# Reordered first loads, head rows written after a logarithm, and more norm tiles in a gated two-layer block

## The chip, the cores and the metric

The kernel runs on one core of a Trainium2 chip. The metric is the device time of one execution in microseconds (us), and the median of several executions is compared. A core has five engines that run side by side, each with an instruction stream of its own that it takes in order: TensorE (PE in the profile, with its weight loads as PEld), VectorE (DVE), ScalarE (ACT), GpSimd (POOL) and SyncE (SP). SP, ACT and POOL can also issue DMA transfers, each into a queue of its own; 16 DMA engines do the moving for all of them.

## What is computed

The input x has 32 samples of 128 tokens with 128 features, and so has the context. Four updates are added to x one after the other, each behind a layer norm:

```
x = x + tanh(g_xattn[0]) * mlstm(layernorm(x), ctx, ctx, ifgate_w, ifgate_b, outnorm_w)
x = x + tanh(g_ffn[0])   * quantized_ffn(layernorm(x), W1, b1, W2, b2)
x = x + tanh(g_xattn[1]) * time_warp_align(ctx, layernorm(x))
x = x + tanh(g_ffn[1])   * gated_experts(layernorm(x), gate_weight, w1, b1, w2, b2)
```

Only the first one matters here. Its gates and its decay matrix are

```
pre    = 15 * tanh((concat[q, k, v] @ ifgate_w.T + ifgate_b) / 15)     # i_pre, f_pre for 8 heads
lf     = cumsum(log_sigmoid(f_pre))
log_d  = lf[t] - lf[s] + i_pre[s]            for s <= t, else -inf
d_mat  = exp(log_d - max_s log_d)
h      = (q k^T / 4 * d_mat) v / max(|row sum|, exp(-m))
```

q is the normed x, and k and v are both the context, so the gate weights of k and v can be summed first.

## The kernel before

The token (or the feature) lies on the 128 partitions; X holds x with tokens on partitions, CT the context in the same way, CD the context with features on partitions, and YT the transposed normed x. Each of X, CT and CD is 2 MB and is loaded in four quarters of eight samples (512 KB each) by `quarter` (L91). So X0 stands for the quarter with samples 0 to 7, X1 for 8 to 15, and so on.

**Loads (L94 to L115).** SP issues X0, CD0, X2, CD2, then CT0, CT1, CD3, CT2, CT3, and then eight small or middle-sized parameters. ACT issues gx (the two gates of the attention updates), X1, wg (the gate weights), gb (the gate biases), gf (the two gates of the feed-forward updates), CD1 and X3. POOL issues none of the first loads.

**Constants.** GpSimd fills masks and small rows; `later_constants` (L129) makes rev, ones, onesb and magic_c. VectorE adds the gate weights of k and v into wkv (L375). ACT takes the tanh of gx and gf (L142, L144), copies an identity pattern to ind (L353), and writes W (L377) from wg and wkv and rows (L382) from gb. TensorE turns the rows into the bias columns cols (L390, L395) and forms the 0/1 head rows hrow (L401, L405).

**Norm.** `norm_steps` (L192) takes n samples: statistics with one BATCH_NORM_STATS2 for each sample (L154), combination and three Newton steps for the reciprocal root (L159 to L189), then for each sample a normed tile y (L210, four tile buffers) that TensorE transposes (L214). After four samples the transposed group is copied to YT (L366 in the first norm, where two groups share a tile of PSUM). `first_norm(0)` does samples 0 to 15, `first_norm(1)` samples 16 to 31.

**Gates.** `gate_steps(r)` (L428) does 16 samples: gate products of W with CD and YT (L437), two tanh (L442), Exp (L443), Ln (L445), a scan for the cumulative sum (L450), g (L455), a scan for the running maximum (L458), a split of the maximum and of g into bf16 parts (L412 to L418, L470), and a DMA of the maximum to DRAM (L464). RH[r] is the right-hand side of the decay product. Four copies, one for each of four samples, fill it with hrow (L407 for r = 0, before the gates; L635 for r = 1, after all steps of the gates), and then `running_max(r)` (L421) overwrites three of its rows in each group of 32 by four DMAs from DRAM, two on SP and two on POOL.

**Attention.** For each sample n, `scores` multiplies CD with qm (L508; qm is YT masked per head, L498), `decays` multiplies GP with RH (L524) and takes the exponential (L529), and `values` multiplies both (L551) and applies them to va (L554). The gates of samples 16 to 31 and the weights' quantization run beside the first samples, a step at a time, through `paced(rest_of_gates())`. `with tc.issue_after(ins)` puts what is written in the block behind `ins` in the order of that instruction's engine; otherwise the tile framework fixes each engine's order at compile time from the order of the program and its own estimate of when an operand is ready.

Of the kernel before, what the change touches and what calls it, by code (L numbers as in the profile page):

```python
# [8 lines left out]
F32 = mybir.dt.float32  # L9
# [9 lines left out]
P = 128  # L19
B = 32  # L20
S = 128
D = 128
NH = 8
# [5 lines left out]
GB = 4  # L29
# [9 lines left out]
def tile_flamingo_gated(  # L39
# [21 lines left out]
    nc = tc.nc  # L61
# [5 lines left out]
    def new(p, shape, dt, tag, bufs=None):  # L67
        kw = {} if bufs is None else {"bufs": bufs}
        return p.tile(shape, dt, tag=tag, name=tag, **kw)
# [5 lines left out]
    X = new(keep, [P, B, D], F32, "X")  # L75
    CT = new(keep, [P, B, D], F32, "CT")
    CD = new(keep, [P, B, S], F32, "CD")
    wg = new(keep, [P, 3, 2 * NH], F32, "wg")
    gb = new(keep, [P, 2 * NH], F32, "gb")
    onw = new(keep, [P, D], F32, "onw")  # L80
    gx = new(keep, [P, 2], F32, "gx")
# [9 lines left out]
    def quarter(queue, to, src, q):  # L91
        queue.dma_start(out=to[:, 8 * q : 8 * q + 8, :], in_=src[:, 8 * q : 8 * q + 8, :])

    for q in (0, 2):  # L94
        quarter(nc.sync, X, x, q)
        quarter(nc.sync, CD, ctx_d, q)
    nc.scalar.dma_start(out=gx, in_=g_xattn.to_broadcast([P, 2]))
    quarter(nc.scalar, X, x, 1)
    nc.scalar.dma_start(out=wg, in_=ifg_w)
    nc.scalar.dma_start(out=gb, in_=ifg_b.to_broadcast([P, 2 * NH]))  # L100
    nc.scalar.dma_start(out=gf, in_=g_ffn.to_broadcast([P, 2]))
    quarter(nc.scalar, CD, ctx_d, 1)
    quarter(nc.scalar, X, x, 3)
    for q in range(4):
        quarter(nc.sync, CT, ctx_t, q)
        if q == 1:
            quarter(nc.sync, CD, ctx_d, 3)
    nc.sync.dma_start(out=onw, in_=outnorm_w.to_broadcast([P, D]))
    nc.sync.dma_start(out=w1s, in_=w1)
    nc.sync.dma_start(out=w2s, in_=w2)  # L110
# [18 lines left out]
    def later_constants():  # L129

        nc.gpsimd.memset(rev, 1.0)
        nc.gpsimd.affine_select(
            out=rev, in_=rev, compare_op=ALU.is_equal, fill=0.0, base=1 - P,
            pattern=[[1, P]], channel_multiplier=1,
        )
        nc.gpsimd.memset(ones, 1.0)
        nc.gpsimd.memset(onesb, 1.0)
        nc.gpsimd.memset(magic_c, MAGIC)
# [8 lines left out]
    held = {}  # L147
# [44 lines left out]
    def norm_steps(p, psp, s0, n, take, tag, shape=None):  # L192

        xq = X[:, s0 : s0 + n, :]
        m, w = (8, "") if n <= 8 else (16, "_w")
        mean = new(p, [P, m], F32, "bn_mean" + w)[:, 0:n]
        r = new(p, [P, m], F32, "bn_r" + w)[:, 0:n]
        for _ in row_norm_steps(p, xq, n, mean, r):
            yield
        for h in range(n // GB):  # L200
            if shape is None:
                tp = new(psp, [P, GB, S], F32, tag)
            else:
                if h % 2 == 0:
                    pair = new(psp, shape, F32, tag)
                tp = pair[:, h % 2]
            for i in range(GB):
                j = GB * h + i
                y = new(p, [P, D], F32, "y", bufs=4)
                got = nc.vector.tensor_scalar(  # L210
                    y, xq[:, j, :], mean[:, j : j + 1], r[:, j : j + 1], ALU.subtract, ALU.mult
                )
                held["y"] = getattr(got, "ins", got)
                nc.tensor.transpose(tp[:, i, :], y, ident)  # L214
                if i % 2 == 1:
                    yield
            take(s0 // GB + h, tp)
            yield
# [70 lines left out]
    with ExitStack() as st:  # L289
        ap = pool(st, "attn")  # L290
        gp = pool(st, "gates")
# [39 lines left out]
        for k in range(2):  # L331
            nc.gpsimd.affine_select(
                out=mtmp[:, k], in_=mtmp[:, k], compare_op=ALU.is_ge, fill=0.0, base=-64 * k,
# [3 lines left out]
                out=mtmp[:, k], in_=mtmp[:, k], compare_op=ALU.is_ge, fill=0.0,  # L337
# [7 lines left out]
            out=mneg, in_=mneg, compare_op=ALU.is_ge, fill=-BIG, base=0,  # L345
            pattern=[[0, 4], [1, P]], channel_multiplier=-1,
        )
        small_c = new(ap, [P, 1], F32, "small_c")
        nc.gpsimd.memset(small_c, 5e-8)
        later_constants()  # L350

        ind = new(ap, [NH, NH, S], BF16, "ind")
# [3 lines left out]
        RH = [new(ap, [P, NH, GB, S], BF16, f"RH{r}") for r in range(2)]  # L356
# [14 lines left out]
            sel[:, :, 0:3, :],  # L371
            identb[0:NH, 0:NH].unsqueeze(1).unsqueeze(1).to_broadcast([NH, R4, 3, NH]),
        )
        wkv = new(gp, [P, 2 * NH], F32, "wkv")
        nc.vector.tensor_add(wkv, wg[:, 1, :], wg[:, 2, :])  # L375
        for k, w in enumerate((wg[:, 0, :], wkv)):
            nc.scalar.copy(  # L377
                W[:, k, :, 0:24].rearrange("p f (c h) -> p f c h", h=NH),
# [19 lines left out]
        hrow = new(gp, [P, NH, S], BF16, "hrow")  # L398
        for k in range(2):
# [3 lines left out]
                rhs=ind[:, 4 * k : 4 * k + 4, :], start=True, stop=True,  # L403
            )
            nc.scalar.copy(hrow[:, 4 * k : 4 * k + 4, :], hr_ps)  # L405
        for i in range(GB):
            nc.scalar.copy(RH[0][:, :, i, :], hrow)  # L407

        def three_parts(v, out_to):

# [10 lines left out]
        def running_max(r):  # L421
            for j in range(R4):
                (nc.sync, nc.gpsimd)[j % 2].dma_start(
                    out=RH[r][HW * j + 24 : HW * j + 27].rearrange("k h i t -> k (h i t)"),
                    in_=m_dram[r, HW * j : HW * j + 24].rearrange("(k h) i t -> k (h i t)", h=NH),
                )

        def gate_steps(r):  # L428

            sp = new(gp, [P, GB * S], F32, "sp", bufs=2)  # L430
            th = new(gp, [P, GB * S], F32, "th", bufs=2)
            for f, to, bias in ((1, sp, bias_f), (0, th, bias_i)):
                ps = new(p_at, [P, GB * S], F32, "at")
                for k, src in ((1, CD), (0, YT)):
                    for j in range(R4):
                        b = 16 * r + 4 * j
                        nc.tensor.matmul(  # L437
                            ps[HW * j : HW * j + HW, :], lhsT=W[:, k, f, :],
                            rhs=src[:, b : b + 4, :].rearrange("p b s -> p (b s)"),
                            start=(k == 1), stop=(k == 0),  # L440
                        )
                nc.scalar.activation(to, ps, AF.Tanh, bias=bias, scale=1.0 / 15.0)  # L442
            nc.scalar.activation(sp, sp, AF.Exp, scale=-15.0)  # L443
            yield
            got = nc.scalar.activation(sp, sp, AF.Ln, bias=one_c)  # L445
            held["Ln", r] = getattr(got, "ins", got)
            yield

            cs = new(gp, [P, GB * S], F32, "cs", bufs=2)
            nc.vector.tensor_tensor_scan(  # L450
                cs, first0.rearrange("p i t -> p (i t)"), sp, 0.0, ALU.mult, ALU.add
            )
            yield
            g = th
            nc.vector.scalar_tensor_tensor(g, th, 15.0, cs, ALU.mult, ALU.add)  # L455
            yield
            mx = sp
            nc.vector.tensor_tensor_scan(  # L458
                mx, firstn.rearrange("p i t -> p (i t)"), g, -BIG, ALU.add, ALU.max
            )  # L460
            yield
            for _ in three_parts(mx, MP[:, r, :]):
                yield
            nc.sync.dma_start(out=m_dram[r].rearrange("p i t -> p (i t)"), in_=MP[:, r, :])  # L464
            if r == 0:
                running_max(0)
            gx3 = new(gp, [P, GB * S], F32, "gx3")
            for _ in three_parts(g, gx3):
                yield
            got = nc.vector.tensor_scalar(GP[:, r, :], gx3, keep24, neg3, ALU.mult, ALU.add)  # L470
            held["GP", r] = getattr(got, "ins", got)
            yield

            nc.vector.tensor_sub(cs, cs, mx)
            yield
            em_ps = new((p_bi, p_at)[r], [P, GB, P], F32, ("bi", "at")[r])
            for i in range(GB):
                nc.tensor.transpose(em_ps[:, i, :], cs[:, S * i : S * i + S], ident)
            yield
            nc.scalar.activation(  # L480
                EM[:, r].rearrange("p i j c -> p (i j c)"),
                em_ps.rearrange("p i c -> p (i c)"), AF.Exp,
            )
# [147 lines left out]
        def rest_of_gates():  # L631
            for _ in second:
                yield True
            for i in range(GB):
                nc.scalar.copy(RH[1][:, :, i, :], hrow)  # L635
                yield True
            running_max(1)
            nc.vector.tensor_scalar(gain, onw, 1.0, tgx[:, 0:1], ALU.add, ALU.mult)
            yield True
            for _ in weight_steps(hp, p_at, "at"):  # L640
                yield True
# [215 lines left out]
    with ExitStack() as st:  # L857
# [51 lines left out]
        for r0, n in CHUNKS:  # L909
            dc = new(wp, [H2, 16, S], F32, "dc")[:, 0:n, :]  # L910
            for v in (slice(0, 4), slice(4, n)) if r0 == 0 else (slice(0, n),):
                for h in range(2):
                    queues[h].dma_start(
                        out=dc[B * h : B * h + B, v], in_=d_dram[h, :, r0 + v.start : r0 + v.stop, :]
# [22 lines left out]
            for q in range(2):  # L937
                for h in range(2):
                    queues[h].dma_start(
                        out=rb[H2 * q + B * h : H2 * q + B * h + B, 0 : m + 1],  # L940
                        in_=ru[B * h : B * h + B, q * m : q * m + m + 1],
# [25 lines left out]
            for q in range(2):  # L967
                queues[q].dma_start(
                    out=DV[:, r0 + q * m : r0 + q * m + m, :], in_=dv[H2 * q : H2 * q + H2]
# [208 lines left out]
```

## Time and profile before

| | us |
|---|---|
| Median of 3 runs | 926.87 (925.89 to 928.11) |
| Profiled execution, its own time | 924.18 |
| Its span | 922.5 |
| First memset to the first decay product (L524) | 51.36 |
| End of the first Ln (L445) | 33.37 |
| Attention stage, to the last YT copy | about 200 |
| Dense and distance stages | about 200 to 318 |
| Time-warp stage | about 318 to 440 |
| Experts | about 440 to 922 |
| One head-row copy (L407 or L635) | 1.04 |

The page gives the busy share of each engine (PE 75%, DVE 62%, ACT 42%, POOL 2%) over the whole span. The stages have different limits, so a share says little about one place; the windows and the timeline of the first 80 us say more.

### The profile page before, as it was taken

The page shows a single profiled execution, that of the slowest core. Times are in us where ns is not written, and L with a number is a line of the kernel's source. Part 1 is how long each engine was busy: PE and PEld are TensorE (multiplying, and loading weights), DVE is VectorE, ACT ScalarE, POOL GpSimd, SP SyncE. Part 2 cuts the span into 40 slices and gives each one's busy share as a digit, 9 for nine tenths or more (in the row PEclk, how much of TensorE's full clock was granted, in tenths as well). Part 3 has the DMA queues.
Part 4 walks back from the last instruction along what each step waited for, and adds up shares of the span by engine and source line. Part 5 has one row for each costly group of instructions (what it writes and reads, how often), then busy time and mean ns, then how long its engine had stood idle before and what let it go on. Part 6 is the DMA issues. An engine that isn't in the chain of part 4 may idle for free.

```text
span 922.5 us, 11329 instructions
## 1 busy us (share of the span) xinstructions
PE 690.1 (75%) x4026; PEld 443.6 (48%) x4026; DVE 568.5 (62%) x1987; ACT 384.7 (42%) x647; POOL 18.0 (2%) x50
## 2 busy tenths in 40 slices
PE   3699999624266400001999999999999999999998
PEld 1223333211044300001777776777777777777776
DVE  5857888869988399978656355897322322322232
ACT  3667665469365300000434444433443343344332
POOL 2000000000400000000000000000000000000000
PEclk9789999855557755555899999999999999999999
DMA  8000000040002435410000000000000000000000
GB/s 303 33 2 11 1 1 1 0 183 0 0 1 47 88 80 111 91 31 0 1 1 1 1 1 1 1 12 24 1 1 12 1 12 1 1 12 1 12 1 12
DMA packets 12081, 25.25 MB, mean 27 GB/s; under 512 B 2528, under 2 KB 7392, under 8 KB 11232
## 3 DMA queue, kind: packets, MB, share of 16 engines
q1 hardware_dynamic: 9448, 18.62, 6.8%
q10 hardware_dynamic: 2448, 5.81, 2.5%
q8 instruction: 31, 0.51, 0.2%
q14 instruction: 26, 0.21, 0.1%
q0 software_dynamic: 128, 0.10, 0.0%
HBM read 14.02 MB, written 4.46 MB: 20 GB/s over the span
## 4 chain that ended last, share of the span: by engine, by line
PE 51%; DVE 22%; issue 2%; ACT 2%; DMA 1%; ACTq 0%; DVEq 0%; POOLq 0%
PE mpo L1108 24%; PE mph L1099 21%; DVE ru L929 3%; DVE hit L975 2%; DVE hst L754 2%; DVE hst L755 2%; DVE ru L928 2%; DVE bn L154 1%; PE d L823 1%; PE po L809 1%; PE d L825 1%; PE small L1039 1%; DVE pt L1023 1%; PE px L1026 1%; PE px L1035 1%
## 5 line engine op out<-in xcount | busy, mean ns | idle before, releaser
L1108 PEld LDWEIGHTS mpo<-mw2s,hT 128*128 128x128 f32 x2048 | 252.2, 192 | 62.6 <-issue 39.2
L1102 ACT ACTIVATE hT<-mph,mb1s 128x512 f32<-128x512 f32 x256 | 175.9, 687 | 237.6 <-PE mph L1099 236.0
L1108 PE MATMUL mpo<-mw2s,hT 128*128 128x128 f32 x2048 | 256.4, 276 | 0.1
L1099 PE MATMUL mph<-YT,mw1s 128*128 128x512 f32 x512 | 243.1, 597 | 0.0
L1087 DVE SCALAR_TENSOR_TENSOR X<-mpo,GA,X 128x128 f32<-128x128 f32 x192 | 54.0, 343 | 198.1 <-PE mpo L1108 198.1
L1099 PEld LDWEIGHTS mph<-YT,mw1s 128*128 128x128 f32 x512 | 87.6, 192 | 61.6 <-issue 61.5
L1087 DVE SCALAR_TENSOR_TENSOR X<-mb2s,GA,X 128x128 f32<-128x128 f32 x256 | 73.1, 342 | 0.0
L882 PE MATMUL gt_ps<-ident,ru 32*128 32x32 f32 x1 | 0.3, 283 | 79.5 <-DVE ru L929 79.5
L551 DVE TENSOR_TENSOR sm<-sc,dm 128x512 f32<-128x512 f32 x64 | 43.6, 684 | 17.3 <-ACT dm L529 17.3
L529 ACT ACTIVATE dm<-bi 128x512 f32<-128x512 f32 x64 | 37.9, 597 | 30.3 <-PE bi L524 24.1
L508 PE MATMUL sc<-qm,CD 64*128 64x512 f32 x128 | 41.3, 652 | 0.0
L882 PEld LDWEIGHTS gt_ps<-ident,ru 32*128 32x128 f32 x1 | 0.2, 178 | 79.6 <-issue 79.6
L965 ACT COPY dv<-vv 128x8 bf16<-128x8 bf16 (+1 forms) x5 | 1.1, 220 | 79.8 <-DVE vv L961 79.8
L554 PE MATMUL at<-sm,va 128*32 128x128 f32 x512 | 28.5, 287 | 5.0 <-DVE sm L551 3.7
L929 DVE TENSOR_TENSOR_SCAN ru<-ru,dc 64x128 f32<-64x128 f32 x64 | 26.7, 417 | 6.7 <-DMA dc<-d_dram 4.7
L745 PE MATMUL ph<-XQ,w1q 128*128 128x512 bf16 x32 | 15.8, 615 | 17.2 <-ACT HT L750 7.7
L523 PE MATMUL bi<-mneg,identb 128*128 128x512 bf16 x64 | 25.7, 401 | 1.9 <-ACT dm L529 1.5
L809 PE MATMUL po<-w2q,hqt 128*128 128x128 bf16 x128 | 13.0, 280 | 17.9 <-DVE hqt L804 17.9
L1036 ACT COPY YT<-px 128x512 f32<-128x512 f32 x8 | 4.7, 585 | 50.5 <-PE px L1035 50.5
L803 ACT ACTIVATE hqt<-HT,low 128x2048 bf16<-128x2048 f32 x8 | 15.8, 1998 | 22.9 <-DVE low L700 13.3
L524 PE MATMUL bi<-RH,GP 32*128 32x512 bf16 x64 | 24.7, 388 | 0.0
L554 PEld LDWEIGHTS at<-sm,va 128*32 128x32 f32 x512 | 10.6, 108 | 29.2 <-DVE sm L551 9.1
(303 smaller groups left out, 843.5 us busy)
## 6 DMA issues: line engine op xcount, KB each, us to landing
CT<-in_ctx_t SPq DMA_DIRECT2D x4, 512.0 KB, 7.6
mw1s<-in_mw SPq DMA_DIRECT2D x1, 2048.0 KB, 8.0
mw2s<-in_mw SPq DMA_DIRECT2D x1, 2048.0 KB, 13.5
out_x<-X SPq DMA_DIRECT2D x8, 256.0 KB, 2.0
d_dram<-dist SPq DMA_DIRECT2D x15, 128.0 KB, 2.4
rblk<-ru ACTq DMA_DIRECT2D x6, 297.0 KB, 4.1
rblk<-ru SPq DMA_DIRECT2D x6, 297.0 KB, 4.8
CD<-in_ctx_d SPq DMA_DIRECT2D x3, 512.0 KB, 8.1
```

The lines of the kernel that those rows point to most:

```text
L508: nc.tensor.matmul(scs[:, k], lhsT=CD[kr, n, :], rhs=qm[kr, :, n % GB, :], start=True, stop=True)
L523: nc.tensor.matmul(bi, lhsT=identb, rhs=mneg, start=True, stop=False)
L524: nc.tensor.matmul(bi, lhsT=GP[jr, r, S * i : S * i + S], rhs=RH[r][jr, 4 * hf : 4 * hf + 4, i, :], start=False, stop=True,)
L529: done = nc.scalar.activation(dm, bi, AF.Exp)
L551: got = nc.vector.tensor_tensor(sm, held["sc", n][:, hf], held.pop(("dm", n, hf)), ALU.mult)
L554: last = nc.tensor.matmul(at[HW * c : HW * c + HW, 2 * (n % 2) + hf, :], lhsT=va[:, n % 8 * NH + 4 * hf + c, :], rhs=sm[:, c, :], start=Tr ...
L809: nc.tensor.matmul(po[:, i, :], lhsT=hq[:, c, i * S : (i + 1) * S], rhs=w2q[:, c, :], start=(c == 0), stop=(c == NC - 1),)
L929: nc.vector.tensor_tensor_scan(ru[:, r + 1, 0, 1 : S + 1], u, dc[:, r, :], BIG, ALU.min, ALU.add)
L1087: nc.vector.scalar_tensor_tensor(X[:, b, :], v, gate, X[:, b, :], ALU.mult, ALU.add)
L1099: nc.tensor.matmul(ph, lhsT=mw1s[:, e, c * P : (c + 1) * P], rhs=tok, start=True, stop=True)
L1102: nc.scalar.activation(hT[:, c, :], ph, AF.Gelu_apprx_tanh, bias=mb1s[:, e, c : c + 1])
L1108: nc.tensor.matmul(po[:, i, :], lhsT=hT[:, c, i * S : (i + 1) * S], rhs=mw2s[:, e, c, :], start=(c == 0), stop=(c == NC - 1),)
```

## The change

- ACT issues wg, gb, gx and gf first and then X1, and no other load. SP issues X0, CD0, X2, CT0, CD2, CT1, CT2, CT3 and then its parameters as before. POOL issues CD1, X3 and CD3.
- The sum wkv is made by GpSimd instead of VectorE. In the program it stands between POOL's second and third load.
- The copies of hrow into RH[r] stand inside `gate_steps`, tied behind that half's Ln on ACT, for both halves; `running_max(r)` follows the DMA of the maximum in both halves.
- y in `norm_steps` has eight tile buffers instead of four.

```
-    for q in (0, 2):
-        quarter(nc.sync, X, x, q)
-        quarter(nc.sync, CD, ctx_d, q)
-    nc.scalar.dma_start(out=gx, in_=g_xattn.to_broadcast([P, 2]))
-    quarter(nc.scalar, X, x, 1)
     nc.scalar.dma_start(out=wg, in_=ifg_w)
     nc.scalar.dma_start(out=gb, in_=ifg_b.to_broadcast([P, 2 * NH]))
+    nc.scalar.dma_start(out=gx, in_=g_xattn.to_broadcast([P, 2]))
     nc.scalar.dma_start(out=gf, in_=g_ffn.to_broadcast([P, 2]))
-    quarter(nc.scalar, CD, ctx_d, 1)
-    quarter(nc.scalar, X, x, 3)
-    for q in range(4):
+    quarter(nc.scalar, X, x, 1)
+    quarter(nc.sync, X, x, 0)
+    quarter(nc.sync, CD, ctx_d, 0)
+    quarter(nc.sync, X, x, 2)
+    quarter(nc.sync, CT, ctx_t, 0)
+    quarter(nc.sync, CD, ctx_d, 2)
+    for q in range(1, 4):
         quarter(nc.sync, CT, ctx_t, q)
-        if q == 1:
-            quarter(nc.sync, CD, ctx_d, 3)
...
-                y = new(p, [P, D], F32, "y", bufs=4)
+                y = new(p, [P, D], F32, "y", bufs=8)
...
         nc.gpsimd.memset(small_c, 5e-8)
+        quarter(nc.gpsimd, CD, ctx_d, 1)
+        quarter(nc.gpsimd, X, x, 3)
+        wkv = new(gp, [P, 2 * NH], F32, "wkv")
+        nc.gpsimd.tensor_add(wkv, wg[:, 1, :], wg[:, 2, :])
+        quarter(nc.gpsimd, CD, ctx_d, 3)
         later_constants()
...
-        wkv = new(gp, [P, 2 * NH], F32, "wkv")
-        nc.vector.tensor_add(wkv, wg[:, 1, :], wg[:, 2, :])
...
-        for i in range(GB):
-            nc.scalar.copy(RH[0][:, :, i, :], hrow)
...
             held["Ln", r] = getattr(got, "ins", got)
             yield
+            with tc.issue_after(held["Ln", r]):
+                for i in range(GB):
+                    nc.scalar.copy(RH[r][:, :, i, :], hrow)
+                    yield
...
-            if r == 0:
-                running_max(0)
+            running_max(r)
...
             for _ in second:
                 yield True
-            for i in range(GB):
-                nc.scalar.copy(RH[1][:, :, i, :], hrow)
-                yield True
-            running_max(1)
```

## Prediction

> **What bounds the kernel now.** I read the page's busy shares first (TensorE leads with 75% of the span), then the chain that ended last: half of it is the expert stage after 440 us, which no edit touches. The edits lie in the first 77 us, so I read that stretch by windows, by the timeline and by the list of waits.
>
> Windows (us; busy time and count of PE, PEld, DVE, ACT, POOL; TensorE clock, DMA share, GB/s), in two answers:
>
> ```profile
> 0.00:5.00 5.00, 0.00 (x0) 0.00 (x0) 3.31 (x2) 0.00 (x0) 4.37 (x27) 1.00 0.46 97
> 5.00:10.00 5.00, 0.00 (x0) 0.00 (x0) 1.23 (x6) 0.00 (x0) 0.51 (x4) 1.00 0.91 330
> 10.00:15.00 5.00, 0.13 (x1) 0.13 (x1) 3.58 (x21) 3.24 (x8) 0.00 (x0) 1.00 0.97 378
> ...
> 33.37:40.00 6.63, 2.28 (x8) 1.41 (x8) 6.59 (x14) 6.60 (x11) 0.00 (x0) 0.63 0.00 0
> 40.00:51.30 11.30, 10.02 (x23) 3.20 (x22) 5.93 (x19) 3.46 (x6) 1.22 (x2) 0.61 0.07 22
> 51.30:61.00 9.70, 9.70 (x75) 3.00 (x74) 3.31 (x5) 6.33 (x10) 0.00 (x0) 1.00 0.00 1
> 61.00:69.00 8.00, 6.60 (x41) 1.91 (x33) 7.06 (x14) 7.25 (x13) 0.00 (x0) 0.80 0.01 2
> 69.00:77.00 8.00, 7.30 (x63) 2.79 (x62) 7.74 (x17) 7.50 (x12) 0.21 (x1) 0.98 0.05 16
> ```
>
> Until 10 us nothing computes but memsets, and the DMA engines are 91% to 97% busy from 5 us on: the loads bound the start. Then a serial chain runs: norm statistics of samples 0 to 15, four groups of transposes and copies, gates, Ln at 33.37, scans, the head rows' DMA, and the first decay product at 51.36. ACT is full right after Ln (6.60 of 6.63 us) and mostly idle after 40 (3.46 of 11.30).
>
> Timeline (start, us, engine, line, operation; in brackets the idle time before it and what ended it):
>
> ```profile
> 11.38 0.18 DVE L375 TENSOR_TENSOR wkv<-wg 128x16 f32<-128x16 f32 x1 [5.11 <-DMA wg<-in_ifg_w]
> 11.49 0.28 DVE L154 BATCH_NORM_STATS2 bn_w<-X 128x6 f32<-128x128 f32 x1
> ...
> 17.86 0.17 DVE L395 COPY cols<-at 128x6 f32<-128x6 f32 x1 [1.28 <-PE at L390]
> ...
> 19.31 3.88 ACT L407 COPY RH<-hrow 128x1024 bf16<-128x1024 bf16 x4
> ...
> 23.10 0.57 ACT L366 COPY YT<-sc 128x512 f32<-128x512 f32 x1
> ...
> 24.10 1.11 DVE L210 TENSOR_SCALAR y<-X,bn_mean_w,bn_r_w 128x128 f32<-128x128 f32 x4 [2.03 <-PE sc L214]
> ...
> 27.55 0.58 ACT L366 COPY YT<-sc 128x512 f32<-128x512 f32 x1 [0.98 <-PE sc L214]
> ```
>
> VectorE stood 5.11 us behind the sum of the gate weights, with the statistics queued behind it; it lost 1.28 us to the bias columns, which TensorE made late; ACT wrote four head rows while the first transposed group waited; and the third group of y waited 2.03 us for one of four tiles.
>
> **What the Trainium skill says.** "DMA: Bandwidth & Descriptors", section "SWDGE vs HWDGE vs iDMA", says that queues of different issuing engines run on the same 16 DMA engines, so that a third queue brings no bandwidth; its section "Queues, rings and completion order" says that the engines take turns between queues. The trace agrees: gx, 1 KB at the head of its queue, needed 6.2 us to land beside SP's big loads. "ScalarE: Activation LUTs" puts a table load at 1283 ns; the trace has 1.28 us, and no edit adds one, since the moved copies need no table switch here (none stands before them).
>
> **The change part by part.**
>
> *Small loads first.* ACT issued gx, X1, wg, gb, gf, then CD1 and X3 at 7.04 and 10.05, and its first table load came at 10.42, after that last issue. Now it issues four small loads and X1 and is free near 4.5 (gf's issue ended at 4.54). The landings: gx at 0.82 + 6.2 = 7.0; wg by 11.38; gf at 3.88 + 9.3 = 13.2, all behind X1. X1 I put at 10.0, since CD1's issue (7.04) followed gx's landing and X3's (10.05) is the next one held back in that way; X0 at 6.7 likewise, by SP's fourth issue at 6.78. Afterwards wg heads the queue and lands about where gx did, 7.0, and the others a little later; so ACT's setup (tanh, ind, W, rows: 13.23 to 14.99) and the columns come two to four us earlier, and the 1.28 us stall goes. VectorE is free of wkv and takes X0's statistics from 6.8 on; X1's landing is what is late next.
>
> X1 pays for it: three more small loads are ahead of it. Wg cost 1.4 us behind X1, gb and gf together 1.85; all of it would put X1 at 13.2, and a third queue in its own 3.0 us (7.0 to 10.0) adds 1.5: 14.7. If the small ones flow while the first big load starts up, it is 11. I take 12.5; the floor is 10.0, the ceiling of the worst case is below, with the rivals.
>
> *From X1 to Ln.* All sixteen statistics took 11.49 to 14.88, so X1's half takes 1.7: 14.2. From L159 (14.92) to the first y (19.19) is 4.27, less the stall 1.28 is 3.0: first y at 17.2, 2.0 earlier. From the first y to the end of the last YT copy it was 19.19 to 28.13, 8.94 us. Of it the head rows (4 x 1.04) held the first copy from 21.55 to 23.10, 1.55; with eight tiles the y's may run through, 4 x 1.12 = 4.5, and then one group of transposes (0.66), a copy (0.58) and waits between give 6.1. Bounds 6.1 and 7.4; I take 6.4. The last copy then ends at 23.6, 4.5 earlier. The tail to Ln's end (28.13 to 33.37, two tanh, Exp, table load, Ln) is unchanged: 28.9.
>
> *Loads through Pool.* CD1, X3 and CD3 go from ACT and SP to POOL, which is idle from 5.5 on (0.51 us busy in 5 to 10). Its issues took 0.52 each (L423) and landed in 2.9. CD1 is needed at 21.48 before, so 12 or 13 is early enough; X3 and CD3 have until about 22 and 30. In POOL's own order wkv waits for wg, and behind it wait CD3, rev, ones, onesb, magic and the iota; none is read before 30 us. Wkv itself: a POOL TENSOR_TENSOR took 0.19 (L340). SP loses CD3 and gains nothing, so CT and the weights move up. Cost nothing, 0 to 1 for a slower start of POOL's queue. If that cover went, CD1 late would hold the gate products by its own lateness.
>
> *Head rows behind Ln, first half.* Four copies of 1.04, 4.2 us, now stand after Ln, where ACT is full; qm, va, EM and the second norm's YT copies are behind them, and TensorE waits for these. The DMA into the same tile waits for them too, but not last: MP was ready 6.7 after Ln (40.04), the copies 4.2 after it. ACT had about 1.0 us of slack before the YT copy at 42.12, so in the worst order that copy slips by 3.2, and with it the products of the second gates, behind which the first scores stand. Against it, VectorE waited 1.42 and 1.82 for y tiles there: up to 3.2 gained. Not visible before the run; bounds -3.2 and +3.2, and I take 0. Ln to first decay stays 18.0.
>
> *Head rows, second half.* The same 4.2 us move from 69 to 77 into about 61 to 69, both windows over 90% ACT. The total doesn't change; each step queued behind them (scans, GP, gain, weight steps) comes two half samples later; the DMA into RH for samples 16 up has until about 120 (51 plus 15 samples of 4.6, the attention stage's mean). VectorE's 1.3 us wait for that Ln may vanish. -1.3 to +4.2, I take 0. Afterwards running_max(1) issues once MP is there, on SP and POOL with nothing near behind it.
>
> *Eight tiles elsewhere.* In the attention stage VectorE lost 0.5 us to y tiles, in the dense stage none: 0.
>
> Sum: -4.5. The profiled execution took 924.18 (span 922.5), so it would take 919.7; it lies 2.7 below the median of the runs shown, and against that I forecast 926.87 - 4.5 = **922.4**.
>
> **The rivals.**
>
> *ACT chokes behind Ln (slower).* Place: the two Ln's. Price: 3.2 + 4.2 = 7.4 against -4.5, so +2.9: 929.8. It decides once more than 4.5 + 1.85 = 6.35 of the 8.3 us of copies lands on the path. For it: 6.60 of 6.63 and 7.25 of 8.00. Against: 7.8 idle us of ACT after 40, and the same copies blocked ACT before as well.
>
> *X1 comes too late.* The three queues share the engines evenly: before X1 is in, SP has moved X0, CD0, X2, CT0 and CD2 and POOL 1.5 MB, 4.5 MB in all with X1. At 330 to 378 GB/s from about 3.5 us that is 15.4 to 17.1, and with POOL's start-up 17.6: first y at 22.3, the last copy at 28.7, +0.6: 927.4. For it: the DMA share above. Against: wg to gf drained fast.
>
> *No net change.* The earlier start is used up in the attention stage, where each step is tied to a sample: 926.9. Little speaks for it: TensorE is 93% busy from 51 to 100 us, so it would simply begin earlier.
>
> *More.* X1 at 11 and half of the y waits: about 8.5 less, 918.4.
>
> **How the numbers follow.** Main case 0.62, more 0.08, ACT choked 0.10, X1 late 0.14 (half of it slower by over 0.2%, half within), no net change 0.06. About 0.2%, 1.85 us, is what a measurement of this kernel can tell from no change. Faster 0.70, same 0.13, slower 0.17. The range goes from 917.0 (the larger gain and 1.4 below it) to 928.0, which takes in X1 late and leaves out ACT choked and small tails.
>
> **What would show it.** The first statistics near 7 and no wait at wkv; the gap before X0's and X1's statistics gives X1's landing; no idle time before the columns; the first y at 17, the last first-half YT copy ending near 23.6, Ln's end near 29, the first decay product (L524) near 47; the stages after 200 as long as before. The prediction is wrong if the first y is after 20, if L524 lies 20 us or more after Ln, or if the stretch from L524 to 200 us grows by more than 2.

## The result, and the profile after

In executions beside those of the kernel before, the changed kernel takes 0.9962 of its time, with a 95% interval of 0.9944 to 0.998: about 3.5 us less. A second set of runs gave 0.9951 (0.9926 to 0.9976), medians 923.57 against 928.69. The median of the first set, 927.26 against 928.07, can't be read without a word on its spread: 9 of the 20 executions took 938 to 945 us at a mean TensorE clock of 0.841 to 0.849 and are left out of the ratio; the experiments with the second half's copies come back to them.

The profile shown is of an execution from the second set, 923.11 us (span 921.4, mean clock 0.865); it is called *again* below. The profiled execution of before that the prediction summed against took 924.18, at the low end of that kernel's executions (924 to 932). So I profiled before once more, at 928.63 (span 926.9), and compare with both.

**The start did not come earlier.** Windows of the changed kernel (columns as in the prediction: length, then busy time of PE, PEld, DVE, ACT and POOL, then TensorE clock, DMA share, GB/s):

```profile
0.00:5.00 5.00, 0.00 (x0) 0.00 (x0) 3.31 (x2) 1.28 (x1) 4.36 (x24) 1.00 0.55 165
5.00:10.00 5.00, 0.00 (x0) 0.00 (x0) 2.91 (x16) 0.20 (x1) 2.58 (x11) 1.00 0.77 228
10.00:15.00 5.00, 0.58 (x2) 0.50 (x2) 0.89 (x6) 1.62 (x5) 0.00 (x0) 1.00 1.02 400
33.37:40.00 6.63, 2.86 (x9) 1.63 (x10) 6.59 (x13) 6.60 (x9) 0.00 (x0) 0.58 0.01 2
40.00:52.60 12.60, 12.03 (x34) 3.29 (x32) 4.97 (x15) 7.72 (x13) 1.29 (x2) 0.95 0.06 18
```

VectorE now works from 5 to 10 us (2.91 against 1.23), but has next to nothing from 10 to 15 (0.89 against 3.58). After Ln, ACT is as full as it was (6.60 of 6.63). From 40 us to the first decay product TensorE runs nearly at full clock, 0.95, where it had 0.61.

Timeline of the changed kernel (start, us, engine, line, operation; the idle time before it and what ended it in brackets):

```profile
6.17 0.29 DVE L152 BATCH_NORM_STATS2 bn_w<-X 128x6 f32<-128x128 f32 x1
...
9.66 0.20 ACT L140 ACTIVATE tgx<-gx 128x2 f32<-128x2 f32 x1 [4.89 <-DMA gx<-in_g_xattn]
...
11.44 0.45 ACT L383 ACTIVATE rows<-gb 1x96 f32<-1x96 f32 x2
...
14.11 0.87 DVE L152 BATCH_NORM_STATS2 bn_w<-X 128x6 f32<-128x128 f32 x4 [6.16 <-DMA X<-in_x]
14.90 0.16 DVE L373 COPY sel<-identb 8x96 bf16<-8x96 bf16 x1
...
15.76 0.58 ACT L406 CAST hrow<-at 128x512 bf16<-128x512 f32 x1 [3.87 <-PE at L402]
...
17.68 0.17 DVE L396 COPY cols<-at 128x6 f32<-128x6 f32 x1 [0.98 <-PE at L391]
...
19.00 0.23 ACT L378 COPY W<-wkv 128x48 f32<-128x48 f32 x1
...
19.84 2.65 DVE L208 TENSOR_SCALAR y<-X,bn_mean_w,bn_r_w 128x128 f32<-128x128 f32 x10
...
20.91 1.92 PE L436 MATMUL at<-CD,W 128*32 128x512 f32 x2
...
22.75 0.69 PE L212 MATMUL sc<-ident,y 128*128 128x128 f32 x2
...
23.48 0.59 ACT L369 COPY YT<-sc 128x512 f32<-128x512 f32 x1 [4.25 <-PE sc L212]
...
27.41 0.58 ACT L369 COPY YT<-sc 128x512 f32<-128x512 f32 x1 [0.93 <-PE sc L212]
```

X0's statistics come at 6.17 and no longer stand behind wkv. Then VectorE waits 6.16 us for X1. The little copy sel, which TensorE needs for the head rows, stands behind X1's first four statistics in VectorE's order, so hrow comes at 15.76 (before: 15.94) and the bias columns at 17.68 (before: 17.86). The first y comes at 19.84, later than before (19.19), the last first-half YT copy ends at 27.99 (before: 28.13), and the first Ln starts at 32.65, to the hundredth where it started before.

The change has a cost here that goes with the sum wkv. GpSimd has wkv ready at 6.11, yet ACT's copy of it into W comes at 19.00, where it came at 14.41 before: the framework has put it behind the second hrow. It does so in all six profiles with wkv on GpSimd (15.65 to 21.07, against 14.24 to 15.54 in the seven with wkv on VectorE). So TensorE stands idle for 1.76 us ahead of the first transposes, where before it did two gate products of CD (at 18.59), and does these two at 20.91, between the transposes of the first group. *notloads*, an experiment with the old loads and wkv on VectorE, but with the copies moved and eight tiles, shows the difference:

```profile
18.42 1.92 PE L434 MATMUL at<-CD,W 128*32 128x512 f32 x2
...
21.42 0.59 ACT L366 COPY YT<-sc 128x512 f32<-128x512 f32 x1 [2.31 <-PE sc L214]
```

There the first YT copy comes 2.41 us after the first y (19.01), in *again* 3.64 us after it. No run moves the sum without the loads, so that it is the sum is argued from the lines and not shown.

### The profile page after: what moved, and what is told of

It reads as the page before. It is cut to its first block, busy times and chain, and to the rows that moved or that the text cites. A ratio compares the mean times of both kernels' runs of the same rounds, so it can differ in the third digit from the quotient of the medians.

```text
span 942.8 us, 11327 instructions
## 1 busy us (share of the span) xinstructions
PE 711.9 (76%) x4019; PEld 450.0 (48%) x4026; DVE 568.4 (60%) x1986; ACT 384.8 (41%) x647; POOL 20.1 (2%) x54
## 4 chain that ended last, share of the span: by engine, by line
PE 50%; DVE 21%; issue 2%; ACT 2%; DMA 1%; ACTq 0%; DVEq 0%
PE mpo L1106 23%; PE mph L1097 20%; DVE ru L927 3%; DVE hit L973 2%; DVE hst L752 2%; DVE hst L753 2%; DVE ru L926 2%; PE d L821 1%; DVE bn L152 1%; PE po L807 1%; PE d L823 1%; PE small L1037 1%; DVE pt L1021 1%; PE px L1024 1%; PE px L1033 1%
## 5 line engine op out<-in xcount | busy, mean ns | idle before, releaser
L510 PE MATMUL sc<-qm,CD 64*128 64x512 f32 x128 | 53.2, 761 | 0.6 <-ACT YT L369 0.6
L556 PE MATMUL at<-sm,va 128*32 128x128 f32 x512 | 31.4, 317 | 4.2 <-DVE sm L553 3.1
L526 PE MATMUL bi<-RH,GP 32*128 32x512 bf16 x64 | 27.3, 428 | 1.0 <-DVE d L584 0.5
L801 ACT ACTIVATE hqt<-HT,low 128x2048 bf16<-128x2048 f32 x8 | 15.8, 1998 | 23.0 <-DVE low L698 13.4
```

Of the source, the lines that this page charges most:

```text
L510: nc.tensor.matmul(scs[:, k], lhsT=CD[kr, n, :], rhs=qm[kr, :, n % GB, :], start=True, stop=True)
L526: nc.tensor.matmul(bi, lhsT=GP[jr, r, S * i : S * i + S], rhs=RH[r][jr, 4 * hf : 4 * hf + 4, i, :], start=False, stop=True,)
L556: last = nc.tensor.matmul(at[HW * c : HW * c + HW, 2 * (n % 2) + hf, :], lhsT=va[:, n % 8 * NH + 4 * hf + c, :], rhs=sm[:, c, :], start=Tr ...
```

## The experiments

Each is described by its difference from the kernel before or from an earlier experiment. Spans and marks are of one profiled execution, ratios of all.

**The two kernels again.** *again* is the changed kernel without an edit, *before2* the kernel before.

> The changed kernel once more, to see its stages in another execution. Theory A (the new loads cost time, the copies and the tiles earn more than that): X1's statistics begin near 15.8 us again and the first decay product comes 2 to 4 us later than before (53 to 55), so the stretch from there to the end of the attention stage must be 6 to 8 us shorter than the 149 us of before; total ratio 0.996. Theory B (the start itself is earlier in an ordinary execution, and the late X1 belonged to that one execution): X1 at 12 or 13, first decay product near 47, the rest as before; total ratio 0.995.

> The kernel before, unchanged, for a second profile, because its first profiled execution (924.18 us) lies near the low end of its executions. Theory A (its usual time, near 928.5, holds a stretch of half TensorE clock that the first profile has not): the extra 4 us stand between 50 and 80 us, with a mean granted clock near 0.856. Theory B (the extra time is spread over the span, or in the expert stage): every stage about as in the first profile, and the rest evenly spread.

The marks of the profiled executions, us (first y; start of the first Ln; first decay product; end of attention, where ACT writes the first XQ, the quantized input of the dense stage; the first time VectorE rescales HT, that stage's hidden layer; first scan of the time warp; first expert product):

| | y | Ln | decay | att. end | quant. | scan | experts | span |
|---|---|---|---|---|---|---|---|---|
| before | 19.19 | 32.65 | 51.36 | 205.03 | 249.69 | 323.37 | 442.71 | 922.5 |
| before2 | 19.34 | 34.03 | 52.45 | 210.11 | 254.76 | 327.20 | 446.53 | 926.9 |
| again | 19.84 | 32.65 | 52.65 | 207.18 | 251.83 | 322.61 | 441.96 | 921.4 |
| loads | 19.70 | 34.07 | 52.58 | 209.59 | 254.24 | 323.88 | 443.24 | 922.7 |
| tiles | 19.17 | 32.52 | 52.12 | 206.99 | 251.65 | 325.32 | 444.65 | 924.4 |
| lt | 19.88 | 35.67 | 54.79 | 206.13 | 250.78 | 320.86 | 440.21 | 919.7 |
| lt_x1 | 17.56 | 33.34 | 52.46 | 203.80 | 248.46 | 318.62 | 437.95 | 917.4 |
| lt_x1_t | 14.42 | 29.31 | 48.18 | 200.08 | 244.74 | 318.66 | 437.98 | 917.5 |

What follows: two executions of the kernel before differ by 4 us in the attention stage alone (153.67 and 157.66 from the first decay product to its end). Against before2 the changed kernel is 5.5 us shorter: 1.4 to the first Ln, 1.5 from there to the end of attention, 1.7 from there to the first scan, 0.9 after it. Against the first profile of before, attention ends 2.2 us later, and the whole gain of 1.1 us comes after it. Neither comparison has the 4.5 us at the start that the prediction summed. Behind 65 us TensorE's half clock lasts 3.4 us in the first profile of before and 10.2 in before2; 6.8 us more of it lose at most 3.4 us (an estimate from these two lengths), which is most of the 3.7 us by which the stretch from the first Ln to the end of attention is longer in before2.

**loads: the new loads, and wkv on GpSimd, alone.** Against the changed kernel, the tiles and both halves' copies (with the second running_max) go back to where they were:

```
-                y = new(p, [P, D], F32, "y", bufs=8)
+                y = new(p, [P, D], F32, "y", bufs=4)
...
+        for i in range(GB):
+            nc.scalar.copy(RH[0][:, :, i, :], hrow)
...
-            with tc.issue_after(held["Ln", r]):
-                for i in range(GB):
-                    nc.scalar.copy(RH[r][:, :, i, :], hrow)
-                    yield
```

> Before with the new order and queues of the loads and with wkv on Pool; copies and tiles as before. Theory A: slower than before by 1 to 3 us (ratio 1.001 to 1.003), X1's statistics near 15.8, first y near 21.5, first decay product near 54. Theory B: faster by 2 to 3 us, first y near 17.

Ratio 0.9955 (0.9938 to 0.9972), median 925.05. This part alone carries a gain of the size of the whole, yet not at the start: up to the end of attention it keeps step with before2 (209.59 against 210.11). What is shorter is the stretch from the first HT to the first scan, 69.64 against 72.44. Neither theory told it so: the start is late, as A had it, and the total is short, as B had it. The list of waits of before2 and then of the changed kernel has two rows there that differ (engine, tile, line, what it waits for: us in all, times, longest):

```profile
DVE ru L929 <- DMA dc<-d_dram: 4.8, 1, 4.8
```

```profile
DVE ru L927 <- DMA dc<-d_dram: 3.0, 1, 3.0
```

The first scan's wait for the distances from DRAM is 4.0 to 4.8 us in all seven profiles with the old loads and 2.6 to 3.0 in all six with the new ones. From the issue of the last distances' store to the first scan it is 7.7 us in before2 and 6.2 in the changed kernel, so it is the transfer that is shorter, but that is about 1.5 us and not the whole gain of loads. Why first loads in the first 10 us should shorten a transfer at 320 us, no run tells. In loads, again, lt and lt_x1 ACT also waits some 1.4 us less before its last distances (6.4 or 6.5 us in two waits against 7.8), but in lt_x1_t it waits 9.3; that part varies.

**tiles: eight y tiles alone.**

```
-                y = new(p, [P, D], F32, "y", bufs=4)
+                y = new(p, [P, D], F32, "y", bufs=8)
```

> Before with eight tile buffers for y in the norms, nothing else. Theory A: faster by 1 to 3 us, all before the first decay product. Theory B: VectorE's waits for y vanish, but TensorE's order sets the pace: within 1 us of before.

Ratio 0.9971 (0.9957 to 0.9986), median 926.07: the edit that I had put at nothing is worth 2.7 us by itself (1.3 to 4.0 by the interval), though not all before the first decay product, as Theory A had it. Where it acts first is between 35 and 50 us, in the second half's transposes. Windows of before2 and then of tiles:

```profile
35.00:50.00 15.00, 9.36 (x23) 3.45 (x24) 11.84 (x30) 8.78 (x14) 1.22 (x2) 0.66 0.05 16
```

```profile
35.00:50.00 15.00, 12.79 (x33) 3.51 (x32) 9.01 (x21) 8.42 (x13) 1.22 (x2) 0.89 0.05 16
```

TensorE gets 12.79 us of work in these 15 us instead of 9.36, and its mean clock is 0.89 instead of 0.66. All seven profiles with eight tiles have 0.77 to 0.98 there, and the six with four tiles 0.54 to 0.66. In the first half twelve y's now run in one row (3.17 us), but the groups of transposes still follow each other 1.5 us apart (a copy of 0.58 to YT and 0.93 to 0.98 of waiting), because two groups share one PSUM tile. Against before2 the first decay product moves by 0.3 us only, the end of attention by 3.1. How much of the 2.7 us the clock makes is not separated: the first profile of before had 0.54 there, with 11.00 us of work, and a short attention stage all the same.

**copies: both halves' head-row copies behind Ln, alone.** In copies1 only the first half's copies stand there (`if r == 0`), in copies2 only the second half's (`if r == 1`), with its `running_max`.

```
-        for i in range(GB):
-            nc.scalar.copy(RH[0][:, :, i, :], hrow)
...
+            with tc.issue_after(held["Ln", r]):
+                for i in range(GB):
+                    nc.scalar.copy(RH[r][:, :, i, :], hrow)
+                    yield
```

> Before with the head rows' copies behind Ln in both halves and running_max in both; loads, wkv and tiles as before. Theory A: faster by 3 to 5 us (ratio 0.995 to 0.997): the first transposed copy is 1.5 us earlier, and the second half's steps stall the attention less. Theory B: first copy 1.5 us earlier, and that is all, or lost again behind Ln: within 2 us of before. If ACT chokes behind Ln: slower, by up to 7 us.

Five of six executions took 943.6 to 946.9 us and one 928.06, so there is no ratio.

> Before with only the first half's head-row copies moved behind its Ln; the second half's stay where they were. Theory A (the second half's copies, behind the second Ln, are what starved TensorE in the run of both copies): within 2 us of before, near 928, and TensorE's half-clock stretch behind 65 us as short as before (3 to 10 us). Theory B (the first half's copies are to blame, by a later first Ln): near 944, with half clock from 67 to about 110.

> Before with only the second half's head-row copies moved behind its Ln (and running_max with them); the first half's stay before the gates. Theory A: near 944 like both copies together, with half clock from 67 to about 110. Theory B: near 928.

copies1: 0.9976 (0.9948 to 1.0004), median 926.15: no loss; the interval takes in both no change and a gain as large as that of tiles. copies2: **1.0158** (1.0137 to 1.018), median 944.78, all four executions above 941. Moving the second half's copies costs about 15 us by the ratio and 16 by the medians, and the windows show that it isn't ACT's queue that loses them. First before2, then copies2:

```profile
60.00:65.00 5.00, 3.60 (x29) 1.31 (x21) 2.66 (x4) 4.94 (x7) 0.00 (x0) 1.00 0.00 0
...
70.00:75.00 5.00, 5.00 (x27) 1.92 (x21) 4.88 (x10) 3.03 (x5) 0.00 (x0) 0.50 0.08 26
75.00:110.00 35.00, 33.73 (x263) 11.94 (x259) 27.76 (x84) 25.56 (x48) 1.03 (x2) 0.98 0.01 4
```

```profile
60.00:65.00 5.00, 2.66 (x19) 0.83 (x15) 1.64 (x2) 4.96 (x7) 0.00 (x0) 0.87 0.00 0
...
70.00:75.00 5.00, 5.00 (x17) 1.12 (x17) 4.72 (x9) 4.05 (x8) 1.03 (x2) 0.50 0.13 44
75.00:110.00 35.00, 34.53 (x160) 11.43 (x160) 15.43 (x44) 14.34 (x28) 0.00 (x0) 0.58 0.01 1
```

Between 75 and 110 TensorE is busy throughout in both, but in copies2 at 0.58 of its clock, with 160 matmuls instead of 263; ACT and VectorE have half their work, since they wait for it. Half clock lasts from 63.7 to 104.7 us there, 41.0 us, and from 65.9 to 76.2 in before2. What the edit changes just ahead of it can be seen in the timelines of before2 and copies2:

```profile
61.81 0.72 ACT L445 ACTIVATE sp<-sp,one_c 128x512 f32<-128x512 f32 x1
62.44 0.57 ACT L561 COPY ats<-at 128x512 f32<-128x512 f32 x1
...
63.06 0.42 PEld L570 LDWEIGHTS at<-ident,ats 128*128 128x128 f32 x4 [0.44 <-ACT ats L561]
```

```profile
60.51 0.72 ACT L445 ACTIVATE sp<-sp,one_c 128x512 f32<-128x512 f32 x1
61.13 1.03 ACT L451 COPY RH<-hrow 128x1024 bf16<-128x1024 bf16 x1
...
62.07 0.57 ACT L565 COPY ats<-at 128x512 f32<-128x512 f32 x1
62.66 1.28 ACT L533 ACT_TABLE_LOAD   x1
62.70 0.42 PEld L574 LDWEIGHTS at<-ident,ats 128*128 128x128 f32 x4 [1.39 <-ACT ats L565]
```

A copy of 1.03 us now stands between Ln and the copy ats, and ats and the table load for the exponentials stand behind it. TensorE waits 1.39 us for ats instead of 0.44, and gets 2.66 us of work in 60 to 65 instead of 3.60. But the gap does not start half clock: all thirteen profiles, with the copies moved or not, enter it here, between 59.5 and 68.3 us. What differs is how long it lasts.

The Trainium skill, "TensorE: Matmul & The Clock Gate", section "Part 1: The HAM clock gate", says that the clock is halved after an idle window of about 3.4 us and full again after a busy one. The lengths fit windows of 3.4 us: 3.4 us in the first profile of before, 10.2 in before2, 41.0 in copies2, that is 1, 3 and 12 of them; the others are 1 and 2, and 13 in copies. The start does not fit an idle window: in the 3.4 us ahead of half clock TensorE has 1.97 us of work in copies2 and 2.01 in before2, and in none of the thirteen do they hold a gap longer than 1.25 us. That the clock should stay low for twelve windows, with TensorE busy for 34.53 of the 35 us from 75 to 110, does not fit either, and no run here explains it. As an estimate from the two lengths, 30.8 us more at half clock than in before2 lose at most 15.4 us of TensorE's work, so this stretch can make the whole loss.

That the long stretch belongs to the second half's edit, the counts show. Of the 81 executions of the six experiments that keep them in their old place, none took more than 930.82 us. Of the 59 of the four kernels that move them, 20 took 938 to 947: 5 of 6 in copies, 4 of 4 in copies2, 2 of 22 in notloads (next), 9 of 27 of the changed kernel. With four y tiles 9 of 10 executions have it, with eight 11 of 49. Counted with them, the changed kernel's mean over its 27 executions is 930.2 us, against 928.3 for before: it gains only in executions without the long stretch. The changed kernel's profile of such an execution has half clock from 67.1 to 108.2, again 41.0 us. In *again* the same copy stands in the same place and TensorE has 2.62 us of work from 60 to 65, but the clock is back after 3.4 us. The gap is thus not enough by itself; what decides is open. One thing goes with it in the five profiles with the copies moved: half clock begins 3.2, 3.4 and 4.0 us after the start of the second Ln where it lasts 41 to 44 us, and 4.9 and 5.6 us after it where it lasts 3.4. Five profiles are too few to call that the reason. Nor is the edit taken apart: running_max(1) moves with the copies (its loads are issued at 73.07 in copies2, behind the start of half clock), and the four copies move together.

**notloads: copies and tiles, without the new loads; lt: new loads and tiles, without the copies.** In lt only the copies go back:

```
+        for i in range(GB):
+            nc.scalar.copy(RH[0][:, :, i, :], hrow)
...
-            with tc.issue_after(held["Ln", r]):
-                for i in range(GB):
-                    nc.scalar.copy(RH[r][:, :, i, :], hrow)
-                    yield
```

> The changed kernel without the new loads: copies behind Ln and eight tiles, loads and wkv as before. Theory A: near the time of eight tiles alone, 926, if the copies are neutral. Theory B (the copies behind the second Ln starve TensorE near 62 to 67 us): 3 us or more above eight tiles alone, with half clock in the windows behind 65 us.

> The changed kernel without the moved copies: new loads, wkv on Pool and eight tiles; head rows where they were before. Theory A (loads and tiles carry the gain, each on its own about 3 to 4 us, the copies nothing): 923 or less, ratio 0.993 to 0.996. Theory B (the gains of loads and tiles are the same few us of TensorE clock, won once): about 925, ratio 0.995 to 0.997.

notloads: 0.9984 (0.9972 to 0.9995). lt: 0.9952 (0.9936 to 0.9968), median 923.29, which is the changed kernel's 0.9951 within the intervals. So the moved copies bring nothing that the intervals show, and the new loads and the tiles bring the gain. Theirs do not seem to add up (0.9955 and 0.9971 would make 0.9926), though that difference is no larger than the three intervals together allow. lt also shows how little the first mark binds: its first decay product comes at 54.79, 2.3 us later than in before2, and its attention ends 4 us earlier.

**lt_x1: X1 on SP.** To learn whether the start carries at all, X1 and CD0 change queues:

```
-    quarter(nc.scalar, X, x, 1)
+    quarter(nc.scalar, CD, ctx_d, 0)
     quarter(nc.sync, X, x, 0)
-    quarter(nc.sync, CD, ctx_d, 0)
+    quarter(nc.sync, X, x, 1)
```

> As lt, but X1 and CD0 change places: X1 is SP's second load, CD0 is ACT's fifth. Theory A (X1's lateness costs what its landing shows, 14.1 us against 10): X1's statistics 4 us earlier, first y near 16, first decay product 3 to 4 us earlier than in lt, total 2 to 4 us less than lt. Theory B (TensorE's order before the first decay product sets the pace): first y earlier, total within 1 us of lt.

Median 921.63, ratio 0.9948 (0.9926 to 0.997). VectorE takes X1's statistics at 7.87 with no wait, though three queues are at work as before. The marks move by 2.3 us at the first y, and by 2.3 at every later mark to the end of the span (917.4 against 919.7). By the medians it is 1.7 us, which the intervals don't tell from none: 13 of the 22 executions of lt_x1 took 918.4 to 922.6 us and nine 925.7 to 929.2, so that one median hides two groups, and no run tells what parts them. The timeline shows why six us of earlier X1 give only 2.3:

```profile
9.74 0.20 ACT L140 ACTIVATE tgx<-gx 128x2 f32<-128x2 f32 x1 [4.92 <-DMA gx<-in_g_xattn]
10.91 0.20 ACT L142 ACTIVATE tgf<-gf 128x2 f32<-128x2 f32 x1 [0.97 <-DMA gf<-in_g_ffn]
...
15.40 0.17 DVE L396 COPY cols<-at 128x6 f32<-128x6 f32 x1 [4.95 <-PE at L391]
```

The columns are late: ACT stands 4.92 us before the tanh of gx, which is first read at 72.2 us, and the first half of W, ind and rows stand behind it.

**lt_x1_t: the two tanh behind the head rows.**

```
-    nc.scalar.activation(tgx, gx, AF.Tanh)
-    nc.scalar.activation(tgf, gf, AF.Tanh)
...
+            got = nc.scalar.copy(hrow[:, 4 * k : 4 * k + 4, :], hr_ps)
...
+        with tc.issue_after(getattr(got, "ins", got)):
+            nc.scalar.activation(tgx, gx, AF.Tanh)
+            nc.scalar.activation(tgf, gf, AF.Tanh)
```

> As lt_x1 (new loads with X1 and CD0 exchanged, wkv on Pool, eight tiles, head rows where they were), and the tanh of gx and gf tied behind the head rows on ACT, since in lt_x1 VectorE waited 4.95 us for the bias columns, whose rows stood on ACT behind these two. Theory A (the columns are the last wait before the first y): columns 2 to 3 us earlier, first y near 15, total 2 to 3 us below lt_x1 (about 919). Theory B (TensorE, still at half clock before the first transposes, or the loads take the gain back): within 1 us of lt_x1.

Median **916.1**, ratio **0.9863** (0.9841 to 0.9886): the best of all, 12.7 us below before, from four executions. Timeline:

```profile
8.94 0.45 ACT L381 ACTIVATE rows<-gb 1x96 f32<-1x96 f32 x2
...
12.26 0.16 DVE L394 COPY cols<-at 128x6 f32<-128x6 f32 x1 [1.82 <-PE at L389]
...
13.57 0.21 ACT L409 ACTIVATE tgx<-gx 128x2 f32<-128x2 f32 x1
...
14.42 1.89 DVE L206 TENSOR_SCALAR y<-X,bn_mean_w,bn_r_w 128x128 f32<-128x128 f32 x7
```

The rows come 3.2 us earlier than in lt_x1, the first y 3.1, the first decay product 4.3 and the end of attention 3.7. The profiled execution was the slowest of the four (919.2; the others 915.2 to 916.4) and gives its 3.7 us back before the first scan, where ACT waits 9.3 us before its distances, 2.9 more than in lt_x1. So the marks show some 4 us of the step from lt_x1; the rest of the 5.5 us between the medians may be that none of these four fell into lt_x1's longer group.

## Why the prediction was right or wrong

The figure was right: faster, by 3.5 to 4.6 us by the two ratios, where 4.5 was summed. The mechanism was not: the start gained nothing, and what was put at nothing made the time. That the sum hit the figure is luck, and it holds only for executions without the long stretch at half clock.

- **Small loads.** X0's statistics came at 6.17 (predicted 6.8), and the rows at 11.44 (14.54 before), in the range of two to four us earlier. The step that failed is "the columns come two to four us earlier, and the 1.28 us stall goes". The columns came 0.2 us earlier and 0.98 of the stall stayed. I followed ACT's setup but not sel, which VectorE puts behind X1's first statistics, nor gx, which as third of its queue landed 7.9 us after its issue.
- **X1.** Landed at 14.1, inside my bounds, 1.6 after my value. A third queue made it neither as late as the rival's 17.6 nor did the small loads let it through in 12.5. lt_x1 shows that with three queues at work it can be there by 7.87, as SP's second transfer; what of the delay is the later issue (2.71 instead of 1.26) and what the other queues was not separated.
- **First y.** 19.84 against 17.2: 1.7 from the statistics, which end later with X1, and 1.0 from the columns.
- **First y to the last YT copy.** 8.15 against 6.4, outside the bounds of 6.1 to 7.4. The head-row copies did hold the first YT copy: without them it comes at 21.42 in notloads, near the 21.55 of the sum. In the changed kernel another wait took their place, which goes with wkv on GpSimd: the two gate products of CD (1.92 us) now stand between the first group's transposes, and the copy comes at 23.48 instead of 23.10. That wkv costs nothing on GpSimd left out where ACT's copy of it would land. Nor does an early first copy give 6.4: in notloads the last YT copy ends 8.0 us after the first y, since gate products (1.94 us) come ahead of the second group's transposes, and afterwards the shared PSUM tile paces the groups at 1.5 us, with four tiles or eight. So Ln ended at 33.37 and not at 28.9.
- **Loads through GpSimd.** Nothing was seen to wait for CD1, X3 or CD3, as predicted, though CD's two took 12.2 us to land (median) and not 2.9.
- **Head rows, first half.** From Ln's end to the first decay product it took 19.28, 1.3 more than the 18.0 that I took, inside the bounds. copies1 shows no loss in the total.
- **Head rows, second half.** Put at 0, bounds -1.3 to +4.2. Where the clock recovers it is 0 (lt against again). By itself it is about +15 us, and a third of the changed kernel's executions pay about as much. The step counted ACT's time and the steps queued behind it and had no term for TensorE's clock. That is where the sum was mis-sized.
- **Eight tiles elsewhere.** Put at 0; alone they are worth 2.7 us. I looked for waits for y tiles in the attention stage. The effect is in the second half's norm beside it, where TensorE is kept at work.
- **Rivals.** ACT choked: the wait behind Ln grew by 1.3 of the 3.2 us priced; the second price came as clock, not as queue. X1 too late: its nine quarters are 4.72 MB and not 4.5, so that its landing should read 16.0 to 17.8; it landed at 14.1, but the last YT copy ended at 27.99, near this rival's 28.7 and far from the main case's 23.6. No net change: not reached. More: not by this change; with X1 on SP and the two tanh moved, 916.1.
- **The measures named beforehand.** The first y (19.84, bound 20), Ln to the first decay product (19.28, bound 20) and the stretch to the end of attention (+0.9 on the first profile, bound +2) all stayed inside, while of the marks set for success only the first was met, X0's statistics without a wait for wkv. Such bounds were too loose to tell the mechanism from luck. In the profile of a long execution of the same kernel two of them broke: X1 landed at 15.8 there, the first y came at 21.54, and the stretch to the end of attention grew by 17.8.

What stays open: how the new loads shorten the wait for the distances at 320 us; how eight tiles' 2.7 us divide between the clock at 35 to 50 us and what follows; why half clock lasts 3.4 us in some executions and 41 in others, and which part of the second half's edit makes it long; and what the late copy of wkv into W costs the whole.

## What to carry to other kernels

Before a load is moved forward, follow every operand of the next serial step to its last producer, on each engine: here a small copy behind statistics held the bias columns, and once X1 was early, two tanh that nobody needed yet held them in its place; only with both out of the way did the total fall by 12.7 us. Then look at what the moved work feeds: wkv was ready early on GpSimd, and the copy that reads it was placed late on ACT. When work is shifted on an engine that feeds TensorE, read TensorE's clock beside its busy time, and in several executions: two kernels about equally busy from 75 to 110 us differed by 103 matmuls, and the changed kernel showed the long half clock in 9 of 27 executions. When a kernel's own executions spread by several us, profile it twice before one profile is used as the base of a sum.

## What the runs showed of the hardware

- In all thirteen profiles the half clock of TensorE that begins between 59.5 and 68.3 us lasts a multiple of 3.41 us: 3.4, 6.8, 10.2, 41.0 or 44.4. It begins after stretches of 3.4 us with 1.1 to 2.7 us of work and no gap above 1.25 us, and in the longest ones TensorE is busy nearly throughout (34.53 of the 35 us from 75 to 110).
- A 1 KB load that was third on ACT's queue landed 7.9 us after its issue, 6.2 when it headed the queue.
- The 512 KB of X1 were used at 14.11 us, 11.4 us after their issue began, as ACT's fifth transfer, and by 7.87 us as SP's second.
